# Two graph layers in one kernel: conv1 of the first batch ahead of the filters, its outputs finished by quarters on TensorE

## The chip, the cores and the metric

The kernel runs on one core of a Trainium2 chip. The core's engines work side by side, each through its own list of instructions in order: TensorE (matrix products into PSUM, with a separate load of the stationary operand), VectorE, ScalarE and GpSimd, and SyncE, whose queue here only issues transfers. They wait for one another through semaphores. The metric is the device time in microseconds (us) of one execution; a profile shows one such execution, and the positions quoted are us from the start of its span.

## The reference, cut to what matters

64 graphs of 256 nodes with 256 features pass through two layers, all in float32. What the change touches lies in the first one:

```python
# layer 0, per graph; x is [256 nodes, 256 features], d = 256
h      = relu(bn1(conv1d(x.T, conv1_w)))           # width 1: a 256x256 product
h      = bn2(conv1d(h, conv2_w, padding=8))        # width 17 along the nodes
x_conv = relu(h + x.T).T
s      = x @ w_se.T + b_se                         # 3 features
A      = exp(-|s_n - s_m|^2) * adj
msg    = relu(x @ w_msg.T + b_msg)
x_nmp  = A @ msg
gi, gh = concat(x_conv, x_nmp) @ w_ih.T + b_ih, x @ w_hh.T + b_hh
# a GRU cell from gi, gh and x; x = layernorm(x + result)
# layer 1 (not touched): layernorm, adj @ h, two 256x256 products, relu, layernorm
```

## The kernel before

The graphs are worked in eight batches of eight. The convolution of width 17 is done by a transform along the nodes: node t*16+j lies in slot j, the 16 slots are split by a tree of rotations and sums (VectorE, in the tile `XF`, seen as slots `X`), each resulting pair of slots is multiplied by transformed filters (TensorE, three products in place of four), and the way back is again VectorE. The filters are transformed on the chip in the first batch: `filters` scales a group of filter taps (`ws`, VectorE), turns it (`tT`), multiplies it with a table of cosines (`ps_w`), and ScalarE copies the result into `w2all`, from which it also goes to memory (`w2m`) for the later batches. There are 20 such groups in 6 pieces, whose taps are loaded one piece at a time into two buffers:

```python
        def fetch(i):
            if i < len(pieces):
                c, o0, o1 = pieces[i]
                WT[i] = pool.tile([P, TAPS, o1 - o0], F32, tag="wt", name="wt", bufs=2)
                nc.sync.dma_start(out=WT[i], in_=w2T[c, :, :, o0:o1])

        def scaled(i, starts):

            c, o0, o1 = pieces[i]
            ws = pool.tile([P, 4, TAPS, OB], F32, tag="ws", name="ws", bufs=3)
            n, o = len(starts), starts[0]
            nc.vector.tensor_mul(
                ws[:, :n], WT[i][:, :, o - o0:o - o0 + n * OB].rearrange("p k (b o) -> p b k o", o=OB),
                bn2_row[:, 0, o:o + n * OB].rearrange("p (b o) -> p b o", o=OB).unsqueeze(2)
                .to_broadcast([P, n, TAPS, OB]))
            return ws
# ... cut: turned(), then in filters():
        for i, (piece, starts) in enumerate(groups):
            c = pieces[piece][0]
            if i + 2 < len(groups):
                WS[i + 2] = scaled(*groups[i + 2])
                if groups[i + 2][0] != groups[i + 1][0]:
                    fetch(groups[i + 2][0] + 1)
            if i + 1 < len(groups):
                TT[i + 1] = turned(WS[i + 1], len(groups[i + 1][1]))
            for a, o in enumerate(starts):
                ps = bank("ps_w")
                nc.tensor.matmul(ps[:, :NM * OB], TT[i][:, a, :], tap_sb, start=True, stop=True)
                skip = OB - D % OB if o == D - OB else 0
                pv = ps[:, :NM * OB].rearrange("p (f o) -> p f o", o=OB)
                nc.scalar.copy(W2[0][:, c, :, o + skip:o + OB], pv[:, :, skip:])
            if i + 1 == len(groups) or pieces[groups[i + 1][0]][0] != c:
                for f in range(0, NM, 8):
                    g = min(f + 8, NM)
                    nc.sync.dma_start(out=w2m[f:g, c].rearrange("f p o -> p f o"), in_=W2[0][:, c, f:g, :])
            yield
```

`conv(b)` is a generator; every `yield` gives an estimate of the VectorE time just spent, by which the caller paces it. The beginning of a batch:

```python
        fetch(0)
        fetch(2)
        yield None
        for g in range(0, BG, 2):
            pair = (b * BG + g) // 2
            xn = XN[g]
            xTc = conv_pool.tile([P, C, 2 * N], F32, tag="xTc", name="xTc", bufs=1)
            for c in range(C):
                ps = bank("ps_xTc")
                for j in range(4):
                    nc.tensor.transpose(ps[:, j * P:(j + 1) * P], xn[:, j, c * P:(c + 1) * P], ident)
                nc.scalar.copy(xTc[:, c, :], ps)
            nc.scalar.dma_start(out=xt_dram[pair], in_=xTc)
            fetch(g + 4)
            yield PE_WEIGHT
            yield None
            for o in range(C):
                ps = bank("ps_c1")
                for c in range(C):
                    nc.tensor.matmul(ps, w1[:, c, o * P:(o + 1) * P], xTc[:, c, :], start=(c == 0), stop=(c == C - 1))
                pv = ps.rearrange("p (g t j) -> p j g t", g=2, j=M)
                for j, at in ((0, 0), (8, 1)):
                    nc.scalar.activation(HP[:, j:j + 8, o, g:g + 2, at:at + M], pv[:, j:j + 8],
                                         AF.Relu, bias=bn_shift[0][:, o:o + 1], scale=bn_scale[0][:, o:o + 1])
                yield PE_WEIGHT * 1.7
        yield None
        for j, r in ((0, 8), (8, 0)):
            hv = HP[:, j:j + 8].rearrange("p j c g k -> p (j c g) k")
            for first, op in ((V + r, ALU.subtract), (U + r, ALU.add)):
                nc.vector.tensor_tensor(sl(first, 8).rearrange("p s (r t) -> p (s r) t", t=M),
                                        hv[:, :, 0:M], hv[:, :, 1:M + 1], op)
                yield cost(8)
        yield from split_all(*TREES[0], S)
        yield from butterflies([(S, V, V + 8, 8, True)])

        other = split_u()
        if b == 0:
            yield from other
        STAGE[b] = "products"
        for _ in range(4):
            yield None
        sv, s8, s4 = {}, {}, {}
# todo: eight sets of products (TensorE), each followed by a "take" out of PSUM and by merges (VectorE)
        vector = deque([other])
        share, spent = (39.0 if b == 0 else 61.0) / len(todo), 0.0
        beyond = 1.0 - 0.85 * 5.2 / (share + 2 * cost(2))
        for i, (make, after) in enumerate(todo):
            if i == 4:
                for t in other:
                    yield beyond * t
            take = make()
            yield PE_WEIGHT
            while vector and spent < share * (i + 1):
                t = next(vector[0], None)
                if t is None:
                    vector.popleft()
                else:
                    spent += t
                    yield beyond * t
            take()
            yield beyond * 2 * cost(2)
            if after:
                vector.append(after)
        STAGE[b] = "inverse"
        for steps in vector:
            yield from steps
        sv, s8, s4 = sv[8, 0], s8[4, 0], s4[2, 0]
```

Its end puts x in on VectorE, turns the slots back on TensorE and applies relu on ScalarE:

```python
        for j in range(4):
            stt(sl(U + j, 2, 4), sl(U + 8 + j, 2, 4), s8[j], sl(S2 + j, 2, 4))
            yield cost(2)
            stt(sl(U + 8 + j, 2, 4), sl(U + 8 + j, 2, 4), -s8[j], sl(S2 + j, 2, 4))
            yield cost(2)
        for j in range(8):
            stt(sl(V + j, 2, 8), sl(V + j, 2, 8), sv[j], sl(U + j, 2, 8))
            yield cost(2)
# ... cut
        def channels(q):
            for o in range(C):
                ps = bank("ps_xc")
                for j in range(4):
                    nc.tensor.transpose(ps[:, j * P:(j + 1) * P], X[:, V + 4 * q + j, o * P:(o + 1) * P], ident)
                pv = ps.rearrange("p (j g t) -> p j g t", j=4, g=BG)
                for h in range(2):
                    nc.scalar.activation(
                        xcs[h][:, o].rearrange("p g (t j) -> p j g t", j=M)[:, 4 * q:4 * q + 4],
                        pv[:, :, 4 * h:4 * h + 4, :], AF.Relu)
                yield 1.0

        before = []
        for q in range(4):
            xb = x_by_tiles(b, q)
            nc.vector.tensor_add(sl(V + 4 * q, 4), sl(V + 4 * q, 4), xb)
            yield cost(4)
            yield None
            before.append(channels(q))
            if len(before) > 2:
                yield from before.pop(0)
        for c_ in before:
            yield None
            yield from c_
        for g in range(BG):
            XC[b * BG + g] = (xcs[g // 4], g % 4)

```

A merge works on the real and the imaginary half one after the other:

```python
        for base, t in ((re, t_re), (im, t_im)):
            a, b = halves(base, n, size, False), halves(base, n, size, True)
            tt = temps(t, n, h)
            if same:
                nc.vector.tensor_sub(tt, a, b)
                yield cost(n * h)
                nc.vector.tensor_add(a, a, b)
                yield cost(n * h)
                continue
```

The first batch runs alone with the filters. All tiles of the pool `first`, `w2all` among them, are released at its end, and the tiles of the pool `work` take their place. Then the messages of the first graphs are made, and from there on each graph's gates, messages, distances and second layer are interleaved with the next batch's convolution by `pump`:

```python
    first, total = conv(0), 0.0
    with tc.tile_pool(name="first", bufs=1) as first_pool:
        fl = filters(first_pool)
        next(first)
        next(fl)
        batch_norms()
# ... cut: the constants are loaded here (lone, wms, bse_row, bmsg, brel, brzn, bhh, gb, whh, wrr)
        total += next(first)
        n_groups = 20
        for i in range(n_groups):
            next(fl)
            while total < FRONT * (i + 1) / n_groups and 0 not in STAGE:
                total += next(first) or 0.0
        for _ in fl:
            pass
        nc.vector.tensor_add(brzn[:, :2 * D], brzn[:, :2 * D], bhh)
        nc.gpsimd.tensor_scalar(wrr, wrr, 0.5, None, ALU.mult)
        nc.gpsimd.tensor_scalar(brel, brel, 0.5, None, ALU.mult)
        while STAGE.get(0) != "inverse":
            total += next(first) or 0.0

    work = ctx.enter_context(tc.tile_pool(name="work", bufs=2))
    wih = weight(wihT, 2 * D, 3 * D, "wih", nc.sync, work)
    for k in range(3):
        load(k)
    load_x(0)
    early = [lambda: messages(0), lambda: messages(1), lambda: factors(0), lambda: distances(0), lambda: mask(0),
             lambda: factors(1), lambda: distances(1), lambda: mask(1), lambda: passing(0), lambda: messages(2)]
    mark = total
    for t in first:
        total += t or 0.0
        if early and total > mark + 1.5:
            mark = total
            early.pop(0)()
    for f in early:
        f()
```

```python
def messages(k):                     # shortened
        for m in range(C):
            ps = bank("ps_msg")
            for c in range(C):
                nc.tensor.matmul(ps[:, :D + 4], XT[k][:, c, m * P:(m + 1) * P], wms[:, c, :],
                                 start=(c == 0), stop=(c == C - 1))
            nc.vector.tensor_add(twice[:, m, :, 0:3], ps[:, D:D + 3].unsqueeze(1).to_broadcast([P, 2, 3]),
                                 bse_row.unsqueeze(1).to_broadcast([P, 2, 3]))
            nc.vector.tensor_add(MSG[k][:, m, :], ps[:, :D], bmsg)
        nc.scalar.activation(MSG[k], MSG[k], AF.Relu)

        nc.gpsimd.tensor_mul(sq, st[:, :, 0:3], st[:, :, 0:3])
        nc.gpsimd.tensor_add(ns, sq[:, :, 0], sq[:, :, 1])
        nc.gpsimd.tensor_add(ns, ns, sq[:, :, 2])
        nc.gpsimd.tensor_scalar(twice[:, :, :, 3], ns.unsqueeze(2).to_broadcast([P, C, 2]), -0.5, None, ALU.mult)
        nc.gpsimd.tensor_scalar(ns, ns, -1.0, None, ALU.mult)
```

The order within a graph k of the steady part, where `pump` stands between any two calls:

```python
gates_rz(k, 0); gates_n(k, 0); transposes_h(k - 1); gates_rz(k, 1); passing(k + 1)
factors(k + 2); gates_n(k, 1); project(k - 1); step(up)   # update(k): nn = tanh(..) on ScalarE
distances(k + 2); step(up)                                # two matmuls, then exp on ScalarE
messages(k + 3); step(up); mask(k + 2); aggregate(k - 1)
```

Of the kernel before, what the change touches and what calls it, by code (L numbers as in the profile page):

```python
# [12 lines left out]
F32 = mybir.dt.float32  # L13
# [32 lines left out]
FRONT = 66.0  # L46
# [29 lines left out]
def gnn_two_layers(  # L76
# [38 lines left out]
    def x_by_tiles(b, q):  # L115

        t = conv_pool.tile([P, 4, D], F32, tag="xb", name="xb")
        nc.sync.dma_start(
            out=t, in_=x[b * BG:(b + 1) * BG].rearrange("g (t j) d -> (g t) j d", j=M)[:, 4 * q:4 * q + 4, :])
        return t  # L120
# [8 lines left out]
    tap_sb = const.tile([TAPS * OB, NM * OB], F32)  # L129
    nc.scalar.dma_start(out=tap_sb, in_=tb_dram.ap())  # L130
# [24 lines left out]
    def along_rows(pool):  # L155

        for i, v in enumerate((bn_scale[1], bn_shift[1])):
            ps = bank("ps_row")
            for c in range(C):
                dg = pool.tile([P, P], F32, tag="dg", name="dg", bufs=4)  # L160
                nc.vector.tensor_scalar(dg, ident, v[:, c:c + 1], None, ALU.mult)
                nc.tensor.matmul(ps[:, c * P:(c + 1) * P], ones, dg, start=True, stop=True)
            nc.scalar.copy(bn2_row[:, i, :], ps[:, :D])
# [3 lines left out]
    W2 = {}  # L167

    def filters(pool):
# [38 lines left out]
        along_rows(pool)  # L208
        TT = {}
        WS = {0: scaled(*groups[0]), 1: scaled(*groups[1])}  # L210
        TT[0] = turned(WS[0], 4)
        for i, (piece, starts) in enumerate(groups):
# [7 lines left out]
            for a, o in enumerate(starts):  # L220
                ps = bank("ps_w")
                nc.tensor.matmul(ps[:, :NM * OB], TT[i][:, a, :], tap_sb, start=True, stop=True)
# [67 lines left out]
    def merge(re, im, size, phis, scales, tmp, new):  # L290


        h, n = size // 2, len(phis)
        t_re, t_im = tmp, tmp + n * h
        same = all(abs(x0 - x1) < 1e-12 for s0, s1 in scales for x0, x1 in zip(s0, s1))
        for base, t in ((re, t_re), (im, t_im)):
            a, b = halves(base, n, size, False), halves(base, n, size, True)
            tt = temps(t, n, h)
            if same:
                nc.vector.tensor_sub(tt, a, b)  # L300
                yield cost(n * h)
                nc.vector.tensor_add(a, a, b)
                yield cost(n * h)
                continue

            assert n == 1 and h % 2 == 0
            for j in range(2):
                rho = scales[0][1][j] / scales[0][0][j]
                a2, b2 = sl(base + j, h // 2, 2), sl(base + h + j, h // 2, 2)
                stt(sl(t + j, h // 2, 2), b2, -rho, a2)  # L310
                yield cost(h // 2)
                stt(a2, b2, rho, a2)
                yield cost(h // 2)
        for k, phi in enumerate(phis):
            tan, c, turned = quarter(phi / 2)
            hr, hi = sl(re + k * size + h, h), sl(im + k * size + h, h)
            dr, di = sl(t_re + k * h, h), sl(t_im + k * h, h)
            if turned:
                stt(hr, dr, -tan, di)
                yield cost(h)  # L320
                stt(hi, di, -tan, dr, op1=ALU.subtract)
            else:
                stt(hr, di, tan, dr)
                yield cost(h)
                stt(hi, dr, -tan, di)
            yield cost(h)
            new.append(scales[k][0] + [c * s for s in scales[k][0]])
# [16 lines left out]
    def merges(which, p, tmp, scales):  # L344
# [4 lines left out]
        while True:  # L349
            below = ([1.0], [1.0]) if s == 2 else (scales[s // 2, 2 * n], scales[s // 2, 2 * n + 1])  # L350
            new = []
            yield from merge(re + n * s, im + n * s, s, [levels[-(s.bit_length() - 1)][n]], [below], tmp + n * s, new)
            scales[s, n] = new[0]
# [68 lines left out]

    def conv(b):
# [507 lines left out]
```

## Time and profile before

Three runs took 2311.68, 2315.41 and 2317.05 us; the median is 2315.41. The profiled execution has a span of 2314.6 us and a mean granted TensorE clock of 0.984.

| engine | busy us | share of the span |
|---|---|---|
| TensorE, matmuls | 2225.2 | 96% |
| TensorE, weight loads (overlap the matmuls) | 1456.2 | 63% |
| VectorE | 1685.2 | 73% |
| ScalarE | 766.0 | 33% |
| GpSimd | 468.7 | 20% |

Busy time is the time within instructions; waits are idle time, and the profile names for each what ended it (the releaser). The chain that ended last is followed back from the last instruction, at each step to what released it. A float32 matmul shows as two records, a transpose as one. The first batch alone, up to the first matmul of the gates, takes 190 us; the rest of the span holds the 64 graphs with seven further convolution batches beside them, and a tail of some 25 us after the last batch.

### The profile page before, as it was taken

What the parts mean: (1) busy time and instruction counts of PE and PEld (TensorE: products, weight loads), DVE (VectorE), ACT (ScalarE), POOL (GpSimd) and SP (SyncE); (2) the same over time, 40 slices, a digit from 0 to 9 for tenths busy, and PEclk for the clock granted to TensorE, in tenths of its full rate; (3) what the DMA queues carried; (4) which work ended last, traced back from release to release, by engine and by line L of the source; (5) the groups of instructions that cost most, each with busy time, mean ns of one, the idle gap of its engine ahead of it and who ended that gap; (6) DMA issues with size and microseconds to landing.
All of it is one profiled execution on the core that took longest, in us unless ns stands there. A gap on an engine that the chain in (4) does not pass through costs nothing.

```text
span 2314.6 us, 24215 instructions
## 1 busy us (share of the span) xinstructions
PE 2225.2 (96%) x8262; PEld 1456.2 (63%) x8262; DVE 1685.2 (73%) x3212; ACT 766.0 (33%) x1577; POOL 468.7 (20%) x925
## 2 busy tenths in 40 slices
PE   7879999999999999999999999999999999999996
PEld 4565566666666666666666566665666656666663
DVE  2893998759794788829887498956889398874543
ACT  4514222442224321353224332253223532243332
POOL 1000221312122222202212131221222122121211
PEclk8998999999999999999999999999999999999998
DMA  5543152224323144221532234222433214321100
GB/s 176 156 161 114 59 170 67 85 94 130 118 73 109 50 137 132 74 100 37 169 99 73 101 106 143 75 96 69 136 105 101 94 43 151 113 78 37 46 23 14
DMA packets 211128, 226.66 MB, mean 98 GB/s; under 512 B 22087, under 2 KB 201790, under 8 KB 211006
## 3 DMA queue, kind: packets, MB, share of 16 engines
q1 hardware_dynamic: 188448, 191.14, 26.2%
q10 hardware_dynamic: 22558, 33.99, 4.2%
q8 instruction: 66, 1.08, 0.2%
q14 instruction: 56, 0.46, 0.1%
HBM read 179.22 MB, written 45.88 MB: 97 GB/s over the span
## 4 chain that ended last, share of the span: by engine, by line
PE 69%; DVE 21%; DMA 4%; issue 3%; POOL 2%; ACT 1%; ACTq 0%; SPq 0%; DVEq 0%; POOLq 0%
PE ps_rz L637 14%; PE ps_k L383 12%; DVE XF L103 8%; PE ps_n L649 7%; PE ps_rz L635 7%; PE ps_out L712 6%; PE ps_c L454 5%; PE ps_nmp L619 4%; PE ps_n L647 4%; PE ps_out L724 3%; PE ps_msg L575 3%; DVE w L103 2%; DVE XF L464 2%; DVE bst L654 2%; DMA w<-w2m 2%
## 5 line engine op out<-in xcount | busy, mean ns | idle before, releaser
L103 DVE SCALAR_TENSOR_TENSOR XF<-XF 128x512 f32<-128x512 f32 (+2 forms) x800 | 506.7, 664 | 7.0
L676 POOL TENSOR_SCALAR q<-mv 128x2 f32<-128x2 f32 x64 | 32.1, 502 | 1459.1 <-DVE mv L655 1459.1
L383 PE MATMUL ps_k<-w,XF 128*128 128x256 f32 x1316 | 302.1, 385 | 15.2 <-ACT AT L609 11.6
L383 PEld LDWEIGHTS ps_k<-w,XF 128*128 128x128 f32 x1316 | 248.5, 192 | 64.1 <-ACT AT L609 17.3
L650 DVE TENSOR_TENSOR gn<-ps_n,brzn 128x512 f32<-128x512 f32 x128 | 88.1, 688 | 239.4 <-PE ps_n L649 239.4
L641 ACT ACTIVATE rz<-rz 128x512 f32<-128x512 f32 x128 | 80.7, 631 | 509.9 <-DVE rz L640 509.9
L635 PE MATMUL ps_rz<-whh,xT 128*128 128x512 f32 x512 | 240.8, 592 | 0.0
L637 PE MATMUL ps_rz<-wih,xc 128*128 128x512 f32 x512 | 240.6, 592 | 0.0
L637 PE MATMUL ps_rz<-wih,nmp 128*128 128x512 f32 x512 | 240.6, 592 | 0.0
L712 PE MATMUL ps_out<-wrr,hT 128*128 128x512 f32 x512 | 232.8, 598 | 5.5 <-ACT hT L701 5.5
L640 DVE TENSOR_TENSOR rz<-ps_rz,brzn 128x512 f32<-128x512 f32 x128 | 87.2, 681 | 192.2 <-PE ps_rz L637 192.2
L637 PEld LDWEIGHTS ps_rz<-wih,nmp 128*128 128x128 f32 x512 | 97.3, 190 | 122.5 <-issue 122.5
L637 PEld LDWEIGHTS ps_rz<-wih,xc 128*128 128x128 f32 x512 | 97.2, 190 | 122.5 <-issue 121.5
L712 PEld LDWEIGHTS ps_out<-wrr,hT 128*128 128x128 f32 x512 | 98.1, 192 | 105.2 <-issue 89.6
L580 ACT ACTIVATE msg<-msg 128x512 f32<-128x512 f32 x64 | 40.4, 631 | 353.1 <-DVE msg L579 353.1
L575 PE MATMUL ps_msg<-wms,xT 128*128 128x260 f32 x512 | 134.1, 402 | 12.5 <-DMA adj<-in_adjT_dram 8.1
L635 PEld LDWEIGHTS ps_rz<-whh,xT 128*128 128x128 f32 x512 | 92.2, 190 | 64.5 <-issue 61.2
L647 PE MATMUL ps_n<-whh,xT 128*128 128x256 f32 x512 | 131.6, 379 | 0.0
L649 PE MATMUL ps_n<-wih,xc 128*128 128x256 f32 x512 | 131.4, 379 | 0.0
L649 PE MATMUL ps_n<-wih,nmp 128*128 128x256 f32 x512 | 131.4, 379 | 0.0
L360 DVE TENSOR_TENSOR XF<-XF 128x512 f32<-128x512 f32 (+3 forms) x128 | 125.2, 1004 | 1.8
L454 PE MATMUL ps_c<-xTc,w 128*128 128x512 f32 x256 | 118.1, 604 | 7.6 <-ACT xTc L446 7.6
(105 smaller groups left out, 3486.6 us busy)
## 6 DMA issues: line engine op xcount, KB each, us to landing
w<-w2m SPq DMA_DIRECT2D x105, 768.0 KB, 5.9
xn<-in_x_dram SPq DMA_DIRECT2D x32, 512.0 KB, 4.3
xt<-xTc ACTq DMA_DIRECT2D x32, 512.0 KB, 3.3
xT<-xt SPq DMA_DIRECT2D x64, 256.0 KB, 3.0
adj<-in_adjT_dram SPq DMA_DIRECT2D x64, 256.0 KB, 2.8
x<-in_x_dram SPq DMA_DIRECT2D x64, 256.0 KB, 3.1
xb<-in_x_dram SPq DMA_DIRECT2D x32, 512.0 KB, 4.9
out_dram<-y ACTq DMA_DIRECT2D x64, 256.0 KB, 2.2
```

What stands on the lines that cost most here:

```text
L103: nc.vector.scalar_tensor_tensor(o, in0, s, in1, op0=op0, op1=op1)
L360: (nc.vector.tensor_add if add else nc.vector.tensor_sub)(sl(o, n), sl(a, n), sl(b, n))
L383: nc.tensor.matmul(ps, X[:, slot, c * P:(c + 1) * P], w(m, c), start=(c == 0), stop=(c == C - 1))
L454: nc.tensor.matmul(ps, w1[:, c, o * P:(o + 1) * P], xTc[:, c, :], start=(c == 0), stop=(c == C - 1))
L575: nc.tensor.matmul(ps[:, :D + 4], XT[k][:, c, m * P:(m + 1) * P], wms[:, c, :], start=(c == 0), stop=(c == C - 1))
L619: nc.tensor.matmul(ps[:, d * N:(d + 1) * N], MSG[k][:, m, d * P:(d + 1) * P], AT[k][:, m, :], start=(m == 0), stop=(m == C - 1))
L635: nc.tensor.matmul(prz, XT[k][:, c, q], whh[:, c, 0:2 * D], start=(c == 0), stop=False)
L637: nc.tensor.matmul(prz, t, wih[:, i, 0:2 * D], start=False, stop=(i == 3))
L647: nc.tensor.matmul(pn[:, D:], XT[k][:, c, q], whh[:, c, 2 * D:], start=(c == 0), stop=(c == C - 1))
L649: nc.tensor.matmul(pn[:, :D], t, wih[:, i, 2 * D:], start=(i == 0), stop=(i == 3))
L650: nc.vector.tensor_add(RZ[k][1][:, n, :], pn, brzn[:, 2 * D:])
L712: nc.tensor.matmul(ps, hT[:, c, n * P:(n + 1) * P], wrr[:, c, :], start=(c == 0), stop=(c == C - 1))
```

## The change

For the first batch it changes the order of work. Conv1 of all four pairs of graphs goes in front of the filters, with groups 0 and 1 of the filters only between the later pairs; each pair is folded as soon as its conv1 is done. The transform on VectorE is then spread evenly over the remaining filter groups. The constants are loaded later, behind the sixth piece of taps. After each product set of the first batch its merges follow at once. The outputs are finished by quarters: x is brought into PSUM by products with the identity, the slots are added to it by further products with the identity, and ScalarE applies relu to the sum, so that VectorE adds no x and no bias of the first messages (that is a product with a row of ones). In all batches a merge handles the real and the imaginary half in one instruction. The aim is a shorter first batch.

```diff
-FRONT = 66.0
+CONV_WEIGHT = 103.8
...
+        both = X[:, re:re + 2 * (im - re)].rearrange("p (b s) e -> p b s e", b=2)
+        a, b = both[:, :, :h], both[:, :, h:size]
+        tt = X[:, tmp:tmp + size].rearrange("p (b s) e -> p b s e", b=2)
+        if all(abs(x0 - x1) < 1e-12 for x0, x1 in zip(*scales)):
+            nc.vector.tensor_sub(tt, a, b)
+            yield cost(size)
+            nc.vector.tensor_add(a, a, b)
+            yield cost(size)
...
+    def fold(g0, g1):
+
+        n = g1 - g0
+        for j, r in ((0, 8), (8, 0)):
+            hv = HP[:, j:j + 8, :, g0:g1].rearrange("p j c g k -> p (j c) g k")
+            for first, op in ((V + r, ALU.subtract), (U + r, ALU.add)):
+                o = sl(first, 8).rearrange("p s (c e) -> p (s c) e", c=C)[:, :, g0 * M:g1 * M]
+                nc.vector.tensor_tensor(o.rearrange("p s (g t) -> p s g t", t=M), hv[:, :, :, 0:M], hv[:, :, :, 1:M + 1], op)
+                yield cost(8 * n / BG)
...
+            if b == 0:
+                yield from fold(g, g + 2)
         yield None
- (the fold of all eight graphs, as above, is taken out)
+        if b > 0:
+            yield from fold(0, BG)
...
-        for _ in range(4):
+        for _ in range(4 if b > 0 else 0):
...
-        share, spent = (39.0 if b == 0 else 61.0) / len(todo), 0.0
+        share, spent = 57.0 / len(todo), 0.0
...
+            if after and b == 0:
+                yield from after
+            elif after:
                 vector.append(after)
...
+            def turned_x(q):
+                xb = FIRST["xb"][q] if q < 2 else x_by_tiles(b, slice(q, M, 4))
+                pss = [bank("ps_xc") for _ in range(C)]
+                for o in range(C):
+                    for j in range(4):
+                        nc.tensor.matmul(pss[o][:, j * P:(j + 1) * P], xb[:, j, o * P:(o + 1) * P], ident,
+                                         start=(j == 0), stop=False)
+                return pss
+
+            yield None
+            held = [turned_x(0), turned_x(1)]
+            for q in range(4):
+                yield from second(q)
+                yield from third(q)
+                yield from third(q + 4)
+                pss = held.pop(0)
+                for o in range(C):
+                    for j in range(4):
+                        nc.tensor.matmul(pss[o][:, j * P:(j + 1) * P], X[:, V + q + 4 * j, o * P:(o + 1) * P], ident,
+                                         start=False, stop=(j == 3))
+                for o in range(C):
+                    pv = pss[o].rearrange("p (j g t) -> p j g t", j=4, g=BG)
+                    for h in range(2):
+                        nc.scalar.activation(xcs[h][:, o].rearrange("p g (t j) -> p j g t", j=M)[:, q::4],
+                                             pv[:, :, 4 * h:4 * h + 4, :], AF.Relu)
+                if q < 2:
+                    held.append(turned_x(q + 2))
+                yield None
+            return
...
+            if idle:
+                nc.tensor.matmul(ps[:, :D + 4], ones[0:1, :], bms[0:1, :], start=False, stop=True)
+                nc.scalar.copy(twice[:, m, :, 0:3], ps[:, D:D + 3].unsqueeze(1).to_broadcast([P, 2, 3]))
+                nc.scalar.activation(MSG[k][:, m, :], ps[:, :D], AF.Relu)
+                continue
...
+        next(first)
+        along_rows(first_pool, 1, bn2_row)
+        next(fl)
+        places = 0
+        for t in first:
+            if t is None:
+                places += 1
+                if places > 2:
+                    next(fl)
+                if places == 5:
+                    break
+
+        done, groups = 0.0, 3
+
+        def filter_steps(last):
+            nonlocal done, groups
+            while groups < last:
+                next(fl)
+                groups += 1
+                while done < 48.6 * (groups - 3) / 17 and 0 not in STAGE:
+                    done += next(first) or 0.0
+
+        filter_steps(15)
...
(the constants are loaded here)
...
+        filter_steps(20)
         for _ in fl:
             pass
-        nc.vector.tensor_add(brzn[:, :2 * D], brzn[:, :2 * D], bhh)
+        while 0 not in STAGE:
+            done += next(first) or 0.0
+        FIRST["xb"] = [x_by_tiles(0, slice(q, M, 4)) for q in range(2)]
         nc.gpsimd.tensor_scalar(wrr, wrr, 0.5, None, ALU.mult)
         nc.gpsimd.tensor_scalar(brel, brel, 0.5, None, ALU.mult)
         while STAGE.get(0) != "inverse":
-            total += next(first) or 0.0
+            next(first)
...
     for k in range(3):
         load(k)
+    wih = weight(wihT, 2 * D, 3 * D, "wih", nc.sync, work)
+    bhh = work.tile([P, 2 * D], F32, name="bhh", bufs=1)
+    nc.sync.dma_start(out=bhh, in_=rows[:, R_HH:R_HH + 2 * D].to_broadcast([P, 2 * D]))
+    nc.gpsimd.tensor_add(brzn[:, :2 * D], brzn[:, :2 * D], bhh)
     load_x(0)
-    early = [lambda: messages(0), lambda: messages(1), lambda: factors(0), lambda: distances(0), lambda: mask(0),
-             lambda: factors(1), lambda: distances(1), lambda: mask(1), lambda: passing(0), lambda: messages(2)]
-    mark = total
-    for t in first:
-        total += t or 0.0
-        if early and total > mark + 1.5:
-            mark = total
-            early.pop(0)()
+    early = [lambda: messages(0, True), lambda: messages(1, True), lambda: factors(0), lambda: distances(0), lambda: mask(0),
+             lambda: factors(1), lambda: distances(1), lambda: mask(1), lambda: passing(0), lambda: messages(2, True)]
+
+    for i, t in enumerate(first):
+        for _ in range((i in (1, 2, 4, 6)) if t is not None else 2):
+            if early:
+                early.pop(0)()
```

## The prediction

> **What bounds the kernel now.** I read four views in this order: busy time by stretches of the span, the chain of waits of the first 200 us, TensorE's waits after 190 us, and instruction groups by form for the durations. First the stretches; columns are length, busy us (instructions) of TensorE, weight loads, VectorE, ScalarE and GpSimd, then granted clock, DMA share, GB/s.
>
> ```profile
> 0.00:50.00 50.00, 36.07 (x120) 21.96 (x121) 9.08 (x22) 22.38 (x45) 6.67 (x15) 0.90 0.63 190
> 50.00:100.00 50.00, 38.18 (x139) 25.30 (x138) 45.71 (x57) 27.21 (x59) 0.00 (x0) 0.88 0.57 168
> 100.00:150.00 50.00, 49.57 (x222) 41.27 (x221) 45.15 (x86) 12.55 (x27) 0.00 (x0) 0.99 0.37 124
> 150.00:200.00 50.00, 31.57 (x117) 21.51 (x116) 36.88 (x72) 14.84 (x32) 7.15 (x17) 0.76 0.44 147
> ```
> ```profile
> 452.00:714.00 262.00, 258.24 (x965) 168.75 (x964) 207.02 (x395) 83.87 (x172) 60.08 (x114) 1.00 0.32 102
> ```
>
> A later batch (262 us) keeps TensorE busy for 258 us: it is the bound, and VectorE with 207 us is not. The first 190 us, up to the first gate matmul (L635, at 190.1), are different: TensorE misses some 14 + 12 + 0.4 + 18 us in these four stretches. All the change can win is there, plus the 3 to 4 us that each later batch loses. VectorE does little until 45 us and is nearly full from then to 164 us. The chain of the first 200 us (start, length, what) says what the end of this part waited for:
>
> ```profile
> 83.58 12.52 DMA wt<-in_w2T_dram
> 96.20 0.66 DVE ws L191
> ...
> 110.51 40.83 PE ps_k L383 x188
> 151.36 6.73 DMA wih<-in_wihT_dram
> 158.10 6.48 DMA xb<-in_x_dram
> ```
>
> So three things pass the chain on: VectorE (filter scaling `ws`, transform `XF`), one transfer of filter taps, and loads that can start only at 151.4, when the last product has read `w2all`. VectorE waited for conv1 until 45.6 us, and ScalarE and TensorE lost time to the output of `xTc`:
>
> ```profile
> DVE XF L464 <- ACT XF L457: 29.7, 1, 29.7
> DVE ws L191 <- DMA wt<-in_w2T_dram: 9.3, 3, 3.8
> ```
>
> After 190 us TensorE's waits are (us in total, times, longest):
>
> ```profile
> PE ps_k L383 <- ACT AT L609: 11.6, 14, 1.1
> PE ps_hT L699 <- DVE h L686: 7.2, 2, 4.6
> PE ps_msg L575 <- DVE XF L399: 4.5, 12, 0.5
> ```
>
> **What the Trainium skill says.** "VectorE: DVE Perf Modes", section on the TRN2 errata, gives an fp32 add as (N+151)/0.96 ns. For 256, 512 and 1024 elements that is 424, 691 and 1224; the trace has 421, 686 and 1222. So one 512 op in place of two of 256 saves 0.15 us. "TensorE: Matmul & The Clock Gate", Part 1, says the array runs at half clock until busy for some 3.4 us, and again after an idle window. The trace agrees: eight transposes take 1.94 us at the start and 1.04 us at 20 us. "SBUF — State Buffer", section on the two separate sides, says GpSimd and VectorE with two SBUF inputs exclude each other for a whole instruction. The trace agrees: the 128x2 op L585 takes 0.5 to 0.6 us beside busy VectorE at 166 us, 0.2 us at 187 us.
>
> **Step 1: conv1 first, folded by pairs.** Before, pair 0's conv1 waited on TensorE behind the first filter group, whose taps landed at 11.2 us; conv1 began at 16.95. After, it stands ahead of the filters and begins at 9.4. From there, with this trace's durations: conv1 of a pair 3.5 us, its transposes 1.05, eight filter transposes 1.2, a filter group's four matmuls 2.4, copies on ScalarE about 1.1 per pair. Pair 1 ends at 18.9, pair 2 (behind group 0) at 27.6, pair 3 (behind group 1) at 35.2; the last relu at 36.3, 10 us before the old 46.0. I assume that `xt` goes out in about 3.5 us (median 3.3) and not the 7.0 of the second pair, since the constants no longer fill the queue. The fold costs 16 x 0.65 instead of 4 x 2.26 us (10.4 against 9.05), but 12 of the 16 are done beside conv1. The transform starts at about 40.6 instead of 56.1: -15 us.
>
> **Step 2: filters and transform.** VectorE still sets the pace. From 56.1 to 113.2 it took 57 us, of which 53 busy; after, 53.5 from 40.6 would be 94. But the sixth piece of taps comes behind 6 MB of transformed filters in the same queue. Before, the writes began at 71.8 and this piece landed at 96.2, 24.4 us later. Now the writes begin 14.6 earlier (57.2), so it lands at 81.5; the order on VectorE wants it already at 76. The wait grows from 3.8 to about 5.6. Transform done at 100 instead of 113.2: -13. Products start at 95.7 instead of 110.4.
>
> **Step 3: products and inverse.** TensorE needs 41 us again, 95.7 to 137. VectorE: 28 + 12 merge ops (20.1 us) become 14 + 6 (17.0), and each product is merged at once rather than spread over 39 us. With 5.2 us a product, product 0 available at 101.7 and product 1 at 107, VectorE then never waits; from there 7.2 + 3.4 + 14.9 + 3.4 + 7.2 + 3.4 + 1.3 = 41 us. Last take at 147 instead of 162.7: -16. This is the most the front holds.
>
> **Step 4: from the last take to the first gate.** Before 27.4 us (162.7 to 190.1): butterflies and stt 14, four adds of x 4.9, message and mask ops 3.8, the rest waits. After, VectorE has 16.3 us of work. But others come in:
> - Loads start when products end, at 137. xT and adj of three graphs and wih (3 MB), then bhh; this stage moved 320 to 370 GB/s, so bhh lands near 149. GpSimd adds it to brzn (1.5 to 2 us: 128x1024 took 2.79) *ahead of* the messages' five small ops. Those start at 151, not at 145; st0 at 153.4, distances, exp: mask 0 at 158. VectorE, done with its first eight ops at 151.5, waits 6 us.
> - Quarter 0 at 158.6 to 161.2. TensorE then has, in order, quarter 0, x of quarter 2 (its tile is loaded only when x of quarter 0 was read, 4 to 5 us), and only then the distances of graph 1, for which mask 1 and quarters 1 to 3 on VectorE wait: mask 1 at 169, quarter 3 at 177.
> - An identity matmul is two records of 0.13 us, a transpose one. X and x together are 64 instructions, 16.6 us instead of 4.2; two thirds lie in waits, but passing 0, messages 2 and 16 identity matmuls (1.75 + 2.7 + 4.2) stand between quarter 1 and the gates.
> First gate at 186, xc ready for it at 187.5. So of the 16 us about 12 are given back: -4 at this point.
>
> **Step 5: later batches.** Their TensorE work is unchanged. The merges save some 3 us of VectorE a batch, which buys nothing directly. But the order on TensorE changes: before, two of eight product groups in a batch came straight behind the distances and waited for exp, which ScalarE runs behind a tanh waiting for VectorE (1.12 and 0.54 us in the batch from 452 us on, then 0.21 and 0.48 for messages). In the new order one of the two comes behind the messages (2 us of other work). So about 1.1 + 0.2 us in each of 7 batches vanish: -9; I take -7, as new waits may show.
>
> **Sum**: -4 - 7 = -11 us from 2315.4: 2304.
>
> **Rivals.** (a) *The front's lead survives whole.* If bhh lands early or the GpSimd add is short, step 4 costs 27 us as before and the gates start at 174: 2293. For it: less VectorE work; against: the order on GpSimd, and the new distance-1 chain. (b) *The lead is lost whole*: cold TensorE in step 4 (clock 0.50 at 170 to 182 us before) makes its 20 us of small matmuls nearer 30, or the filter piece stalls for 9 us. Gates at 190 or later: 2308 to 2316. (c) *The later batches turn worse*: product order moves a wait to the last products, which now stand inside the gates of a graph. Seven batches by 1 us: 2311. (d) VectorE's lighter merges help all batches: excluded, as it is idle a fifth of them.
>
> **Range and chances.** Front between -14 and +2, later batches between -10 and +3: 2292 to 2316 holds it 8 times in 10. A 2% gain would be 46 us, about all the idle TensorE time of the front: 0.02. A 2% loss would need a new stall in each batch: 0.01.
>
> **What would show it.** Step 1: last conv1 matmul near 35 us, first 1024-wide XF op near 40. Step 2: one wait of 4 to 8 us for `wt` on VectorE, between 75 and 82. Step 3: products start at 95 and end at 137; the last take near 147. Step 4: GpSimd's brzn add ends near 151 and mask 0 is near 158; gates near 186. Step 5: waits of ps_k for AT down from 11.6 to about 5. Wrong if the taps stall is gone, if the brzn add runs before 146, or if a later batch's length changes by over 2 us.

## The result and the profile after

| | median, us | profiled span, us | mean granted clock |
|---|---|---|---|
| before | 2316.2 | 2314.6 | 0.984 |
| changed | 2383.2 (4 runs, 2374.9 to 2392.6) | 2378.8 | 0.974 |

The ratio is 1.0294, with an interval of 1.0252 to 1.0337: slower, where 2304 was predicted. The first batch came out as predicted; the loss arose in the seven others. First the changed kernel's busy time by stretches (columns as in the prediction):

```profile
0.00:50.00 50.00, 41.24 (x161) 26.60 (x162) 26.11 (x48) 29.90 (x61) 3.05 (x13) 1.00 0.54 152
50.00:100.00 50.00, 37.87 (x148) 25.82 (x147) 41.62 (x65) 26.95 (x60) 3.96 (x2) 0.90 0.69 211
100.00:150.00 50.00, 46.31 (x193) 37.65 (x191) 46.10 (x73) 5.85 (x13) 0.00 (x0) 0.91 0.62 204
150.00:200.00 50.00, 43.92 (x219) 32.24 (x218) 17.72 (x26) 17.11 (x40) 5.87 (x18) 0.85 0.25 83
462.00:724.00 262.00, 252.57 (x931) 166.19 (x930) 202.53 (x371) 78.98 (x161) 64.65 (x113) 0.99 0.31 102
```

VectorE now has work before 50 us, and the last 50 us of the front keep TensorE at 43.92 instead of 31.57. The last line is the surprise: in 262 us of later batches TensorE is busy 252.57 us where it was 258.24, and does 931 matmul records where it did 965. The chain of waits of the first 200 us says that the front itself went by the plan:

```profile
31.99 3.45 PE ps_c L460 x8
...
39.69 2.28 DVE XF L103 x2
...
69.99 12.62 DMA wt<-in_w2T_dram
...
97.21 40.83 PE ps_k L379 x188
142.22 9.37 DMA bhh<-in_rows_dram
151.97 1.56 POOL brzn L883
...
169.43 0.69 DVE AT L662
...
186.30 1.72 PE ps_rz L685 x4
```

The last conv1 ends at 35.4, the products start at 97.2 and GpSimd's add ends at 153.5. The first matmul of the gates (L685) starts at 186.1, where it started at 190.2. So what remains from there to the end is 2378.8 - 186.1 = 2192.7 us, against 2314.6 - 190.2 = 2124.4 before: 68 us more, some 9.7 in each of seven batches. TensorE's waits after 200 us show where (totals, times, longest):

```profile
PE ps_k L379 <- DVE XF L395: 33.5, 7, 4.8
PE ps_k L379 <- DMA w<-w2m: 17.7, 8, 3.0
PE ps_k L379 <- ACT XF L394: 8.8, 7, 1.3
PE ps_hT L749 <- DVE h L736: 6.9, 2, 4.6
PE ps_out L762 <- ACT hT L751: 5.9, 1, 5.9
PE ps_c L460 <- ACT xTc L452: 3.6, 6, 0.6
PE ps_msg L619 <- ACT AT L659: 3.2, 7, 0.5
```

The wait for exp that the prediction meant to remove (`ps_k` for `AT`, 11.6 us) is gone. In its place each batch waits once, up to 4.8 us, for L395, VectorE's first operation of a take (a subtraction that reads PSUM), and about once, up to 3.0 us, for a filter load, for which the kernel before waited little:

```profile
PE ps_k L383 <- DMA w<-w2m: 2.5, 5, 0.7
```

All waits after 230 us sum to 79.6 us, before to 36.0: 43.6 more. The other part is in the products' own duration, changed and before (busy us, then the mean ns of one; matmuls overlap, so that the mean times the number is more than the busy time):

```profile
L379 PE MATMUL ps_k<-w,XF 128*128 128x256 f32 x1316 | 328.7, 410 | 60.0 <-DVE XF L395 33.5
L383 PE MATMUL ps_k<-w,XF 128*128 128x256 f32 x1316 | 302.1, 385 | 15.2 <-ACT AT L609 11.6
```

That is 26.6 us more. 43.6 + 26.6 less 4.1 won in the front is 66.1; the spans differ by 64.2.

TensorE's timeline in one batch puts both parts side by side (start, length, what; in brackets the idle time before and its releaser):

```profile
597.98 1.14 PE L619 MATMUL ps_msg<-wms,xT 128*128 128x260 f32 x4 [0.45 <-ACT AT L659]
598.96 1.89 PE L379 MATMUL ps_k<-w,XF 128*128 128x256 f32 x8
605.64 5.25 PE L379 MATMUL ps_k<-w,XF 128*128 128x256 f32 x16 [4.79 <-DVE XF L395]
...
662.72 6.24 PE L379 MATMUL ps_k<-w,XF 128*128 128x256 f32 x20 [2.29 <-DMA w<-w2m]
```

A product set is 24 matmul records in three PSUM buffers of eight; it fills the first half of each buffer in turn, and then the second halves. The set at 598.96 runs its first eight records, into the first and the second buffer, and then stands for 4.79 us in front of the third. After the gap 16 records take 5.25 us; at the pace of the first eight they would take 3.8. VectorE's timeline says what L395 was behind:

```profile
599.93 0.68 DVE L717 TENSOR_TENSOR w<-x,nn 128x512 f32<-128x512 f32 x1
...
603.19 1.79 DVE L356 TENSOR_TENSOR XF<-XF 128x1024 f32<-128x1024 f32 x2
604.90 0.68 DVE L395 TENSOR_TENSOR XF<-XF,ps_k 128x512 f32<-128x512 f32 x1
```

L395 does not make the input of this set: it writes slots 4 and 5, and the set reads slots 6, 7, 14, 15, 38 and 39. It reads the third buffer of the *preceding* set, and by the allocation in the built program this is the PSUM bank in which the new set's third buffer comes to lie. The Trainium skill, "PSUM — Partial Sum Buffer", section "PSUM: the matmul accumulator", gives eight banks, and a matmul writes to one of them; the built program uses these eight. At this place two hold the node products (`ps_out`), three the preceding set, and distances and messages have taken the rest. Before, the set stood ahead of the messages, and its second and third buffers came to lie in the two banks of the distances. VectorE works through its list in order: ahead of L395 stand the GRU's update (L717 to 603.2) and two butterflies.

The order on TensorE round the distances of a graph, read from the built programs (D distances, M messages, O aggregation and, at the end of a graph, the node products, R and N gates, h turn, P passing, s factors, K a product set, kkk the batch's last set), is in two successive graphs of a batch:

```
before    DKMORRRNNNKhRRRPKsNNNO   DKMORRRNNNkkkhRRRPsNNNO
changed   DMKORRRNNNKhRRRPKsNNNO   DKMORRRkkkNNNhRRRPsNNNO
```

So my theory is one of order and banks: the changed pacing (`share` 57 for 61 and `CONV_WEIGHT` 103.8 for the 107.7 that the old code summed up) moved a set from in front of the messages to behind them, where its third bank comes free only after VectorE's update; and moved the last set before the N gates, where its filters have not landed. (In the graph ahead of these two a further set moved by one place, to behind the turn.) Rivals: the fused merges leave VectorE otherwise loaded and so the take late (the expectations call this MERGE); or something of the new first batch stays on and slows the others. A second part of the first theory, called TAKE in run 5, is that the take is late because it stands behind the update on VectorE.

### The profile page after: what moved, and what is told of

Read it like the earlier page. It is cut to its first block, busy times and chain, and to the rows that moved or that the text cites. A ratio compares the mean times of both kernels' runs of the same rounds, so it can differ in the third digit from the quotient of the medians.

```text
span 2378.8 us, 24309 instructions
## 1 busy us (share of the span) xinstructions
PE 2259.9 (95%) x8370; PEld 1486.9 (63%) x8370; DVE 1672.1 (70%) x3048; ACT 768.3 (32%) x1585; POOL 500.9 (21%) x926
## 4 chain that ended last, share of the span: by engine, by line
PE 83%; DVE 9%; DMA 3%; issue 1%; ACT 1%; POOL 1%; SPq 0%; ACTq 0%; POOLq 0%; DVEq 0%
PE ps_rz L687 16%; PE ps_k L379 14%; PE ps_n L699 9%; PE ps_rz L685 8%; PE ps_out L762 7%; PE ps_c L460 5%; PE ps_nmp L669 5%; PE ps_n L697 4%; PE ps_out L774 4%; PE ps_msg L619 4%; DVE XF L103 3%; DMA w<-w2m 2%; PE ps_dist L657 1%; PE ps_hT L749 1%; PE ps_xc L573 1%
## 5 line engine op out<-in xcount | busy, mean ns | idle before, releaser
L379 PE MATMUL ps_k<-w,XF 128*128 128x256 f32 x1316 | 328.7, 410 | 60.0 <-DVE XF L395 33.5
L726 POOL TENSOR_SCALAR q<-mv 128x2 f32<-128x2 f32 x64 | 65.0, 1016 | 1478.8 <-DVE mv L705 1478.8
L379 PEld LDWEIGHTS ps_k<-w,XF 128*128 128x128 f32 x1316 | 269.0, 207 | 115.9 <-DVE XF L395 36.3
L685 PE MATMUL ps_rz<-whh,xT 128*128 128x512 f32 x512 | 240.7, 592 | 0.0
L619 PE MATMUL ps_msg<-wms,xT 128*128 128x260 f32 x512 | 135.0, 404 | 6.8 <-DMA adj<-in_adjT_dram 3.7
L685 PEld LDWEIGHTS ps_rz<-whh,xT 128*128 128x128 f32 x512 | 92.8, 190 | 64.8 <-issue 61.2
L763 ACT COPY hr<-ps_out 128x256 f32<-128x256 f32 x128 | 47.7, 372 | 234.1 <-PE ps_out L762 234.1
```

Of the source, the lines that this page charges most:

```text
L379: nc.tensor.matmul(ps, X[:, slot, c * P:(c + 1) * P], w(m, c), start=(c == 0), stop=(c == C - 1))
L685: nc.tensor.matmul(prz, XT[k][:, c, q], whh[:, c, 0:2 * D], start=(c == 0), stop=False)
```

## The experiments

Each is one kernel; the kernel before took 2315.6 to 2317.6 us beside them. All ratios are to it.

**1. One set moved back.** Only the set behind the messages goes in front of them again.

```diff
 (changed kernel)
-CONV_WEIGHT = 103.8
+CONV_WEIGHT = 104.5
```

> The changed kernel with one number altered: the pace of the convolution in the later batches is 104.5 instead of 103.8. On TensorE this moves exactly one of the eight product sets of a batch, from behind a graph's messages back to ahead of them. Theory ORDER: behind the messages the products find no free PSUM bank and wait 4.8 us for a take that stands on VectorE behind a graph's update, and the clock halves after the gap. Then 4.8 us and some 1.5 us of half clock vanish in each of 7 batches and 1.1 us of the old wait for exp returns: 2383 becomes about 2345 (2335 to 2355). Rival MERGE: the merges of both halves in one instruction (longer VectorE instructions, which also hold up GpSimd) slow the later batches: no change, 2375 to 2390. Rival FRONT: the new first batch leaves the later ones behind in some way: no change either.

Measured: 2331.6 us, ratio 1.0060 (1.0040 to 1.0081). 51.6 of the 67 us are back, by one changed pacing figure. The wait of `ps_k` for L395 is gone; 7.9 us of it appear at the messages, 13.5 us of the wait for filters remain.

**2. The whole order back.** The sets have their old neighbours; the rest of the change stays. (With the new figures the turns of a batch's outputs stand one place elsewhere, here and in runs 3 and 4.)

```diff
 (changed kernel)
-CONV_WEIGHT = 103.8
+CONV_WEIGHT = 106.6
...
-        share, spent = 57.0 / len(todo), 0.0
+        share, spent = 60.0 / len(todo), 0.0
```

> The changed kernel with two numbers altered (share 60 instead of 57, pace 106.6 instead of 103.8), which puts all products of the later batches between the same neighbours on TensorE as in the kernel before; the first batch and the merges stay as in the changed kernel. Theory ORDER: the later batches cost what they cost before and the first batch keeps its gain of 3.8 us: 2312 (2306 to 2318). Rivals MERGE and FRONT: 2370 to 2390.

Measured: 2310.8 us, 0.9978 (0.9971 to 0.9985). The rival of the new first batch falls: with the new first batch and the old order the kernel is 5 us faster than before. TensorE's waits:

```profile
PE ps_msg L619 <- DVE XF L395: 13.2, 14, 1.5
PE ps_hT L749 <- DVE h L736: 7.2, 2, 4.6
PE ps_k L379 <- ACT AT L659: 7.0, 14, 0.5
```

The bank of L395 is still awaited, but by the messages, twice in a batch and by 0.9 us on average, since a whole product set (about 5 us) lies between.

**3. The order alone, in the kernel before.** Nothing of the change but such an order: the pace is 106.5, where the old code summed up 107.7, so that two sets in each batch stand behind the messages.

```diff
 (kernel before)
-            while done < total * at / goal:
+            while done < 106.5 * at / goal:
```

> The kernel before with one number altered: its pace in the later batches is 106.5 instead of 107.7. This moves two product sets of a batch from ahead of the messages to behind them and nothing else of the products; first batch and merges are those of before. Theory ORDER: each moved set brings a wait of 3 to 5 us for a take, with half clock after it: 2316 becomes 2360 to 2400. Rivals MERGE and FRONT: no change, 2312 to 2320.

Measured: 2396.5 us, 1.0346 (1.0325 to 1.0366), slower by more than the change itself.

```profile
PE ps_k L383 <- DVE XF L399: 60.6, 14, 4.4
PE ps_msg L575 <- ACT AT L609: 8.3, 14, 0.8
```

L399 there is the same add as L395. Two sets moved, 14 waits of 4.3 us; one moved in the changed kernel, seven of 4.8. The old merges and the old first batch are in this kernel, so neither is needed for the loss.

**4. The fused merges alone** (the rival MERGE), with the order kept (the diff of `merge` as in the change, and `share` 60 and pace 106.6 for the order).

> The kernel before with the merges of both halves in one instruction, in all batches, and share 60 and pace 106.6, so that the products keep their neighbours on TensorE. Theory ORDER: some 3 us less VectorE work in a batch buys nothing; 2310 to 2320. Rival MERGE: 2340 to 2385.

Measured: 2318.6 us, 1.0008 (0.9999 to 1.0018). MERGE falls as the cause of the 67 us. Its largest waits after 200 us are those of run 2 to the digit (13.2 and 7.0). Its gates start at 186.3: the lighter merges alone bring the gates as far forward as the whole new first batch does. But no time comes of it: the messages wait for L395 13.2 us where they waited 4.5, while the products wait for exp 7.0 instead of 11.6. Run 2, with its gates at 187.2, is nevertheless 3.9 us shorter in the profiled span and 7.8 in the median. Of the 3.9, 2.9 us are shorter waits of TensorE (for filters 0.4 instead of 2.4, for VectorE's statistics none instead of 1.3); the rest these runs do not show.

**5. The take ahead of the update.** If the set waits because L395 stands behind the update on VectorE, then exchanging the two there, with TensorE's order left as it is, must shorten the wait.

```diff
 (changed kernel, behind the distances)
-            step(up)
             pump()
+            step(up)
```

> The changed kernel with two lines swapped in the later batches: after a graph's distances the convolution goes on first, and only then come the update's last VectorE operations. TensorE's order stays that of the changed kernel; only on VectorE the take of the product set that holds the bank moves ahead of the update (subtraction, two stt, two bn_stats: 3.3 us). Theory TAKE (the bank is freed late because its take stands behind the update on VectorE): the wait of 4.8 us for L395 falls to 1 to 2 us, TensorE stays at full clock, and 2383 becomes 2340 to 2360. Rival BANK ALONE (the position behind the messages costs this wait whatever VectorE does before it, for instance because of the distances' exp on ScalarE): no change, 2375 to 2390.

Measured: 2337.0 us, 1.0094 (1.0079 to 1.0109): 46 us better than the changed kernel, somewhat more than expected. In the same place of a batch:

```profile
594.77 1.89 PE L379 MATMUL ps_k<-w,XF 128*128 128x256 f32 x8
598.34 3.72 PE L379 MATMUL ps_k<-w,XF 128*128 128x256 f32 x16 [1.68 <-DVE XF L395]
```

The gap is 1.68 instead of 4.79 us, and the 16 matmuls behind it take 3.72 instead of 5.25: as expected, TensorE stays at full clock behind this gap. All seven waits for L395 together are 11.8 us instead of 33.5; 3.5 us less waiting for filters (14.2 instead of 17.7) come on top. That L395 holds the set up by the bank is read from the built program; no run changes the allocation alone.

**6. No set between distances and aggregation.** If banks are short only there, sets put elsewhere should wait for nothing.

```diff
 (changed kernel)
-        share, spent = 57.0 / len(todo), 0.0
+        share, spent = 61.0 / len(todo), 0.0
```

> The changed kernel with share 61 in the later batches: every product set stands outside the stretch from a graph's distances to its aggregation, in which the two ps_out banks are held; where the set stood behind the messages it now stands behind the aggregation, which has given two banks back. Theory: no product waits for a take any more, and the waits for exp and for L395 that even the kernel before has (some 3 us a batch) go too: 2290 to 2312. If instead the position of a product set behind the messages or later is bad in itself (operands or filter loads late): 2340 or more.

Measured: 2314.7 us, 0.9995 (0.9987 to 1.0004), just above the expected range. The scarcity only moved on:

```profile
592.95 1.03 PE L379 MATMUL ps_k<-w,XF 128*128 128x256 f32 x4
596.24 6.24 PE L379 MATMUL ps_k<-w,XF 128*128 128x256 f32 x20 [2.27 <-DVE st L626]
```

The set behind the aggregation now waits for L626, VectorE's reader of the messages' bank, 22.9 us in 14 waits of up to 2.3. No product reads what L626 writes, and by the built program's allocation the set's second buffer lies in that bank; so here too it is a bank that is waited for.

**7, 8 and 10. What held the front.** By step 4 of the prediction two things give the front's lead back: GpSimd's `brzn` add ahead of the messages' small ops, and the distances of graph 1 behind the first quarter. All three runs have the order of run 2. Run 7 moves the add behind the first messages; run 8 also brings the distances forward; run 10 brings the distances forward and leaves the add where the change has it.

```diff
 (run 7 and run 8; not in run 10)
-    nc.gpsimd.tensor_add(brzn[:, :2 * D], brzn[:, :2 * D], bhh)
     load_x(0)
...
+    nc.gpsimd.tensor_add(brzn[:, :2 * D], brzn[:, :2 * D], bhh)   (behind the remaining early steps)
 (run 8 and run 10; not in run 7)
-        for _ in range((i in (1, 2, 4, 6)) if t is not None else 2):
+        for _ in range((i in (1, 2, 4, 6, 10)) if t is not None else 2):
```

> As e2_order_back (2310.8), with GpSimd's addition of bhh to brzn moved from ahead of the first messages' small operations to behind them. Theory (step 4: these wait for the landing of bhh): mask 0 comes some 6 us earlier; what of it reaches the gates depends on the distances of graph 1, which still stand behind the first quarter on TensorE: the gates start at 182 to 185 instead of 187, and the time is 2304 to 2310. Rival: the outputs by quarters are bound by TensorE's identity matmuls: no change.

> As e7_brzn_later, with the distances of graph 1 on TensorE ahead of the first quarter of outputs, passing 0 behind it and messages 2 behind the second quarter. Theory: mask 1 and with it quarters 1 to 3 no longer wait for quarter 0 and the x tile of quarter 2: the gates start at 176 to 181, and the time is 2300 to 2306. Rival (identity matmuls bound it): as e7, 2304 to 2310.

> The order of the products as before, distances of step 1 ahead of the last quarter's first turn, the bias add of GpSimd left where the change has it. If both together are needed to win the 6 us (the add delays GpSimd's input work and this the distances' masks), 2309 to 2312. If the distances' place alone did it, 2304 to 2307.

Measured: run 7 2311.2 us (0.9980, 0.9973 to 0.9987), run 8 2305.0 (0.9953, 0.9937 to 0.9969), run 10 2306.7 (0.9953, 0.9941 to 0.9966). The add moved alone brings the gates from 187.2 to 185.4 and gains no time over run 2; the distances alone gain as much as both, within the intervals. The chain of run 10, round the masks:

```profile
141.01 8.83 DMA bhh<-in_rows_dram
150.23 1.50 POOL brzn L883
...
162.78 0.63 PE ps_dist L657 x4
...
179.47 1.72 PE ps_rz L685 x4
```

The add is still on the chain and yet the gates start at 179.3 instead of 187.2 in run 2. The distances of graph 1 run at 162.8 instead of 167.8 in the changed kernel, so that mask 1 starts at 164.4 instead of 169.4, and the quarters behind it on VectorE follow. Of the 7.9 us by which the gates come earlier, 4.1 arrive in the median.

**9. Both ideas together**: run 8 with the exchange of run 5.

> The order of the products as before, the front of the run with distances of step 1 and the wih-side bias add moved, and take ahead of update behind the distances. If the wait of the messages for L395 (13.2 us over 14 in the run without the swap) is of the same cause as the wait that the swap shortened in the changed kernel, it should vanish or nearly: 2291 to 2297. If the messages then wait for the next reader of a bank (exp or the relu), 2300 to 2306. If update now comes too late for something else on VectorE, over 2306.

Measured: 2287.6 us, 0.9874 (0.9859 to 0.9890): 30 us faster than the kernel before, and below what I expected. The wait of the messages for L395 (13.2 us in run 8) is gone:

```profile
PE ps_hT L749 <- DVE h L736: 7.2, 2, 4.6
PE ps_k L379 <- ACT AT L659: 7.0, 14, 0.5
PE ps_out L762 <- ACT hT L751: 5.7, 1, 5.7
PE ps_c L460 <- ACT xTc L452: 3.6, 6, 0.6
PE ps_k L379 <- DMA w<-w2m: 0.5, 2, 0.3
```

In the stretch from 462 to 724 us TensorE is busy 260.70 of 262 us. All waits after 230 us sum to 21.8 us; in run 10, which differs from it in the exchange and in the add's place, to 36.3. The spans differ by 18.5, so some 4 us of the gain appear in no wait. They are busy time: the messages' own 480 matmuls (L619) take 119.1 us instead of 122.8. Why they do stays open.

**11. The exchange in the kernel before.**

```diff
 (kernel before, behind the distances)
-            step(up)
             pump()
+            step(up)
```

> The kernel before with nothing changed but take ahead of update behind the distances. Its messages wait for L399 only 4.5 us in all, so if that wait alone is what the swap can remove, 2310 to 2313. If the swap also brings what it brought behind the changed order (19 us between the two runs with the new front, of which waits explain 14.5), 2295 to 2303. If before is bound there by exp alone (11.6 us of waits), no change: 2314 to 2317.

Measured: 2305.6 us, 0.9953 (0.9940 to 0.9967), between the first two cases. The wait of the messages for L399 (4.5 us) is gone, the 11.6 us for exp are left, and the spans differ by 9.2. Again some 4.7 us of it are busy time and no wait, 3.2 of them in the messages' matmuls (119.8 us instead of 123.0). So one exchanged pair of lines gains about 10 us without the first batch being touched.

## Why the prediction was right or wrong

**Step 1, right.** Last conv1 at 32.0 to 35.4 (predicted near 35), the first large XF op of the transform at 39.7 (40.6).

**Step 2, right in kind.** One wait for the sixth piece of taps, which lands at 82.6 (81.5); VectorE's wait was 7.6 us, not 5.6. Products start at 97.2, not 95.7.

**Step 3, right.** Products 97.2 to 138.0, the last add of a take at 148.4 (predicted last take near 147).

**Step 4, right in time, half right in its reason.** The add ends at 153.5 (151), mask 0 starts at 159.1 (158), mask 1 at 169.4 (169), the gates at 186.1 (186). That the last figure fits so well is in part luck: the add was 2.5 us late, and the stretch from it to the gates 2.4 us shorter than predicted. Runs 7, 8 and 10 show that of the two named causes the place of graph 1's distances counted for most: moved alone, the distances bring the gates 7.9 us forward, the add 1.8 and no time.

**Step 5, wrong in sign and size: this step failed.** It said that "about 1.1 + 0.2 us in each of 7 batches vanish". No wait of `ps_k` for exp is left (11.6 us before), but ScalarE is waited for as long as it was: the set still behind the distances now waits for L394, a copy out of PSUM that stands behind the same tanh, 8.8 us, and the messages wait for exp, 3.2. What failed is the step from the moved set's new place to -7 us. The prediction took it that "2 us of other work" would cover the set's wait. It did not ask why a product waits for exp at all: no product reads what exp writes. By the allocation in the built program, the second and third buffers of that set lay in the two banks of the distances, which exp reads. So the wait on record was already one for a bank, and the moved set had to wait for another bank with a later reader. "I take -7, as new waits may show" allowed 2 us in all; the new waits are 33.5 for L395 and 15.2 more for filters, with 8.8 for L394, and the slower clock behind them. Runs 1, 2 and 3 show that the order alone makes this loss; run 5 shows that L395's place behind the update makes most of it, 46 of the 67 us.

**The rivals.** (c), later batches worse by a wait at the last products, had the direction and part of the place: the last set does wait for filters, up to 3.0 us. It put this at 1 us a batch; the batch lost 9.7, and the larger part lay at a set that (c) did not name. The filter wait is a queue's: the load waits in SyncE's queue behind an `adj` load that is held until the aggregation has read its tile, and is issued at 656.2 for products due at about 660.4; this is read from the order in the trace, and no run moves that load. (d) was rightly excluded: run 4 gained nothing. (a) was not reached, but run 10 shows that 8 of its 12 us at the gates were to be had by the place of one entry in a list, and 4 of them in the time.

**The range** of the later batches, -10 to +3, was the unsound part. The prediction named the sign that would refute it, "a later batch's length changes by over 2 us", and gave a loss of 2%, by "a new stall in each batch", a chance of 0.01, though the diff shows two pacing figures changed for all batches.

## What to carry to other kernels

A figure that only paces an interleaving is a change of program order, and so of the order in which PSUM banks are asked for. For each instruction that moves, ask for its inputs, for the last reader of the bank that its output gets, and for what that reader stands behind on its own engine. Where that reader is an operation of 0.7 us that stands behind 5 us of less urgent work, as here, exchange the two. And where a trace shows a matmul waiting for an instruction whose result it does not read, as for exp here, look whether that instruction read the bank that the matmul writes.

## What the runs showed of the hardware

A gap on TensorE can cost more than its length, because the granted clock may be down behind it. In the changed kernel it is 0.70 over the 5.3 us after the gap of 4.79, 0.80 over the 8.6 us that include the gap of 2.29, and 0.50 over 6.8 us round the end of another gap for L395:

```profile
605.60:610.90 5.30, 5.26 (x17) 4.41 (x18) 4.26 (x11) 1.61 (x3) 3.87 (x8) 0.70 0.00 2
660.40:669.00 8.60, 6.31 (x22) 5.28 (x22) 6.39 (x15) 2.09 (x4) 2.45 (x4) 0.80 0.35 122
1165.13:1171.96 6.83, 6.18 (x15) 4.93 (x16) 4.87 (x12) 1.61 (x3) 4.40 (x9) 0.50 0.01 2
```

Missing clock of 0.30 x 5.3 is 1.6 us, and 0.20 x 8.6 is 1.7: at half speed, some 3.2 to 3.4 us of slow running each time, and twice that in the third line. But the length of the gap alone does not decide. Gaps of one length ahead of the same products came out differently, in the changed kernel (first two lines, against those at 605.64 and 662.72 above) and in the kernel before (last two):

```profile
1165.78 6.76 PE L379 MATMUL ps_k<-w,XF 128*128 128x256 f32 x16 [4.78 <-DVE XF L395]
1224.38 4.55 PE L379 MATMUL ps_k<-w,XF 128*128 128x256 f32 x20 [2.30 <-DMA w<-w2m]
...
865.70 6.27 PE L383 MATMUL ps_k<-w,XF 128*128 128x256 f32 x20 [1.12 <-ACT AT L609]
1410.57 4.58 PE L383 MATMUL ps_k<-w,XF 128*128 128x256 f32 x20 [1.12 <-ACT AT L609]
```

After 4.8 us, 16 records take 5.25 or 6.76; after 2.3 us, 20 take 6.24 or 4.55; after 1.12 us, 20 take 6.27 or 4.58. So these traces give no length below which a gap is safe. The Trainium skill, "TensorE: Matmul & The Clock Gate", Part 1, says that the clock is set by windows of 3413 ns that run freely and do not start with the kernel. The trace agrees: in the later batches the slow stretches last that long or twice that, and three of them, from 322.04, 605.35 and 1165.13 us on, start 83 and 164 times 3.413 us apart. Where a gap falls in the window can then differ from batch to batch. The page also has the clock drop after an idle window of that length; here it dropped behind gaps of 1.12 us, in two of the seven batches of the kernel before.

The mean granted clocks of 0.974 and 0.984 over the whole spans leave 61.8 and 37.0 us of clock missing, an estimate of 25 us more in the changed kernel, close to the 26.6 us that the products grew: the loss of each batch is some six tenths waiting, and the rest the clock behind it.
